# Cross attention of layer 1: one tile of values per chunk, a joint copy of the last chunk, layer norms moved behind a reciprocal

## Chip, cores and metric

The kernel runs on one core of a Trainium2 chip. The metric is the device time of one execution in microseconds. TensorE (PE in the profile, with its weight loads as PEld), VectorE (DVE), ScalarE (ACT) and GpSimd (POOL) each work through their own queue of instructions, and SyncE (SP) issues most of the DMAs.

## What is computed

The reference is a decoder of two layers on 32 sequences of 100 tokens with 256 features. Each layer has self attention, a cross attention to a context of 361 rows with 192 features, and a mixture of experts. The change touches the cross attention of layer 1 alone, and the code of that stage also starts the gating of the following mixture of experts. Cut to what matters:

```python
# x: (32, 100, 256), context: (32, 361, 192); 16 heads of 64
def _L1_xattn_ref(x, context, ln_gamma, ln_beta, Wq, Wkv, Wo, bo, mask):
    xn = (x - mu) * jax.lax.rsqrt(var + LN_EPS) * ln_gamma + ln_beta
    q = xn @ Wq
    k, v = jnp.split(context @ Wkv, 2, axis=-1)
    dots = jnp.einsum('bhnd,bhmd->bhnm', q, k) * scale      # q, k, v by head
    dots = jnp.where(mask, dots, -jnp.inf)
    attn = jax.nn.softmax(dots, axis=-1)
    out = jnp.einsum('bhnm,bhmd->bhnd', attn, v)            # back to (32, 100, 1024)
    return out @ Wo + bo

x = x + _L1_xattn_ref(_layernorm(x, axis=-1), ctx_768, ...)
x = x + _L1_ffn_ref(_layernorm(x, axis=-1), ...)            # experts; its gate reads the normed x
```

Everything is float32.

## The kernel before, in words

The stage works in units. Unit u is one sequence (u // 4) and four of its sixteen heads (u % 4), so there are 128 units. A loop calls `turn_of(n)` for n from -2 to 127, and one turn holds pieces of several units, one behind the other, so that each engine always has something to do. The order on TensorE, VectorE, ScalarE and GpSimd is the order in which the code is written: the stage stands in `in_order()`, which takes the order out of a scheduler's hands. The waits between engines are put in from what instructions read and write.

A turn n is, in order:

- `turn_weights`: twelve transposes of the weights of unit n (`ex`, made two turns earlier) into three `mm` tiles in PSUM, copied to `eT` by ScalarE, VectorE and ScalarE.
- `exponentials` of the second half of unit n + 1 on ScalarE.
- `part_of(n)`: work that isn't needed in every turn. When n is a multiple of 4, `finish` projects the sequence just done and adds it to x (VectorE), then adds a bias (GpSimd) and stores x. In certain turns of each 16 it does the layer norm of the next four sequences (`normed`: part 0 statistics, part 1 centering), their queries (`turned`, `queries`), and the gating of the four sequences just finished (`gating`: part 0 statistics, part 1 centering and a store to `xn_dram`, part 2 transposes, part 3 the gate's projection and the two best experts, part 4 the gates).
- `values(v, last, 0)`: the first half of the sums over the context's features for the values of a pair of units. The 361 rows of context fall into chunks of 128, 128 and 105. In an even turn the first two chunks are made, 512 columns each; in an odd turn (`last`) the third, as two halves of 256 columns. All go into one tile `sc` of PSUM, which has two parts of 512 columns.
- `keys(n + 3, 0)`, and `divided(n + 1)`: a reciprocal on VectorE of the sums of the weights (`rc`), and the multiplication of the weights by it on GpSimd.
- `values(v, last, 1)`: the second half of the sums, and then the copies out of `sc` into the tile `vb`: the first part by ScalarE (L1517), the second by VectorE (L1519).
- `scores(n + 2, 0)`: matmuls into the other of the two `sc` tiles, and VectorE lowers them into `s` with the row's extreme `nmx` (L1538). `keys(n + 3, 1)` with its copies into `kT` by ScalarE (L1484) and VectorE (L1485). `scores(n + 2, 1)`: these take the `sc` tile that the values were in.
- `sums`: 24 short matmuls of `eT` and `vb` into `po`, copied to `oT` by VectorE.

Statistics are four pairs of BATCH_NORM_STATS2 and BATCH_NORM_AGGREGATE and one small operation on VectorE, then a power on GpSimd (`rs`, L170). Centering is four TENSOR_SCALAR on VectorE (L176). PSUM is shared as two `sc` tiles, three `mm` tiles and one `po` tile.

The functions of the diff, with their callers:

Of the kernel before, what the change touches and what calls it, by code (L numbers as in the profile page):

```python
# [10 lines left out]
F32 = mybir.dt.float32  # L11
# [7 lines left out]
P = 128  # L19
# [3 lines left out]
NG = B // G  # L23
# [42 lines left out]
def kernel(ctx: ExitStack, tc: tile.TileContext, io: dict, out: bass.AP):  # L66
    nc = tc.nc
# [22 lines left out]
    def mm_tile():  # L90
        return psum["mm"][1].tile([P, 512], F32, tag="mm", name="mm")
# [29 lines left out]
    def bc(ap, axis, n):  # L121

        ap = ap.unsqueeze(axis)
        shape = list(ap.shape)
        shape[axis] = n
        return ap.to_broadcast(shape)
# [414 lines left out]
    with tc.tile_pool(name="x0", bufs=2) as pool, tc.tile_pool(name="x0p", bufs=1) as fixed:  # L541
# [32 lines left out]
        cbs, cns, cTs, kbs, kns, vbs, kTs, exs, eTs, oTs = {}, {}, {}, {}, {}, {}, {}, {}, {}, {}  # L574
# [188 lines left out]
        def divided(b):  # L763
            ex, sm = exs[b]
            rc = small.tile([T, XH], F32, tag="rc4", name="rc4")
            nc.vector.reciprocal(rc, sm)
            nc.gpsimd.tensor_tensor(ex, ex, bc(rc, 2, NK), ALU.mult)
# [54 lines left out]
        with in_order():  # L822
# [8 lines left out]
            for n in range(-4, B + 1):  # L831
# [18 lines left out]
                g = (n + 5) // G  # L850
# [4 lines left out]
                g = (n + 4) // G + 1  # L855
# [41 lines left out]
    with tc.tile_pool(name="f0", bufs=2) as pool:  # L897
# [40 lines left out]
        parts = {}  # L938
# [16 lines left out]
        def gating(g, part):  # L955
            if part == 0:
                x1T = pool.tile([P, 2, GT], F32, tag="x1T", name="x1T")
                transposed(x1T, x1s[g], tiles=mm_tile)
                pg = mm_tile()
                for i in range(G):  # L960
                    project(
                        pg[:T, i * E : (i + 1) * E],
                        [x1T[:, c, i * T : (i + 1) * T] for c in range(2)],
                        [f0_wg[:, c, :] for c in range(2)],
                    )
                lg = small.tile([T, G, E], F32, tag="lg", name="lg")
                nc.vector.tensor_tensor(
                    lg, pg[:T, : G * E].rearrange("p (g e) -> p g e", e=E),
                    bc(row("f0_gb"), 1, G), ALU.add,
                )  # L970
                nmx = small.tile([T, G], F32, tag="nmg", name="nmg")
                nc.vector.tensor_reduce(nmx, lg, AX.X, ALU.max, negate=True)
                nc.vector.tensor_tensor(lg, lg, bc(nmx, 2, E), ALU.add)
                nc.scalar.activation(lg, lg, AF.Exp)
                x1Ts[g], parts[g] = x1T, lg
                return
            lg = parts.pop(g)
            sm = small.tile([T, G], F32, tag="smg", name="smg")
            nc.vector.tensor_reduce(sm, lg, AX.X, ALU.add)
            nc.vector.reciprocal(sm, sm)  # L980
            gt = small.tile([T, G, E], F32, tag="gt", name="gt")
            nc.vector.tensor_tensor(gt, lg, bc(sm, 2, E), ALU.mult)
            _, hot = top2(pool, gt, G, row("iota", P))
            wt = small.tile([T, G, E], F32, tag="wt", name="wt")
            nc.vector.tensor_tensor(wt, hot[:T, 0], hot[:T, 1], ALU.add)
            nc.vector.tensor_tensor(wt, wt, gt, ALU.mult)
            wts[g] = [wt]
# [90 lines left out]
    with tc.tile_pool(name="a1", bufs=2) as pool, tc.tile_pool(name="a1p", bufs=1) as fixed:  # L1078
# [21 lines left out]
        for c in range(2):  # L1100
            ps = mm_tile()
# [5 lines left out]
        ps = mm_tile()  # L1107
# [213 lines left out]
        with in_order():  # L1321
            for part in range(11):
                project_group(0, part)
            for n in range(16 * NG + 12):
                g, at = n // 16, n % 16
# [79 lines left out]
    with tc.tile_pool(name="x1", bufs=2) as pool, tc.tile_pool(name="x1p", bufs=1) as fixed:  # L1405
# [32 lines left out]
        def normed(g, part):  # L1438
            if part == 0:
                lns[g] = stats(xs[g], G, twice=True, tag="l")  # L1440
            else:
                xn = pool.tile([T, G, D], F32, tag="xn", name="xn", bufs=1)
                centered(xn, xs[g], G, lns[g])
                lns[g] = xn
# [42 lines left out]
        def values(u, last, part):  # L1487

            b, v0 = u // 4, 512 * (u % 4 // 2)
            cT, vb = cTs[b], vbs[u // 2]  # L1490
            if last:
                k0, kn = CCH[2]
                parts = [(slice(k0, k0 + kn), kn, v0 + 256 * e, 256) for e in range(2)]
            else:
                parts = [(slice(k0, k0 + kn), kn, v0, 512) for k0, kn in CCH[:2]]
            if part == 0:
                held[u] = sc_tile()
            ps = held[u]
            for e, (at, kn, c0, n) in enumerate(parts):
                half = slice(64 * e, 64 * e + 64)  # L1500
                if part == 0:
                    nc.tensor.matmul(  # L1502
                        ps[:kn, e, :n], cT[:, 0, at], x1_wa[:, 1024 + c0 : 1024 + c0 + n],
                        start=True, stop=False,
                    )
                else:
                    nc.tensor.matmul(  # L1507
                        ps[:kn, e, :n], cT[half, 1, at], x1_wbv[half, c0 : c0 + n],
                        start=False, stop=True,
                    )  # L1510
            if part == 0:
                return
            for e, (at, kn, c0, n) in enumerate(parts):
                src = ps[:kn, e, :n].rearrange("p (h d) -> p h d", d=64)
                dst = vb[:kn, 2, 4 * e : 4 * e + 4, :] if last else vb[:kn, e, :, :]
                if e == 0:
                    nc.scalar.copy(dst, src)  # L1517
                else:
                    nc.vector.tensor_copy(dst, src)  # L1519

        def scores(u, c):

# [50 lines left out]
        def sums(u, eT, vb, oT):  # L1573

            q4 = u % 4
            po = po_tile()
            for m in range(2):
                for k, (k0, kn) in enumerate(CCH):
                    for e in range(2):
                        h = 2 * m + e  # L1580
                        nc.tensor.matmul(  # L1581
                            po[64 * e : 64 * e + 64, m * T : (m + 1) * T],
                            vb[:kn, k, 4 * (u % 2) + h, :], eT[:kn, k, h, :],
                            start=(k == 0), stop=(k == 2), tile_position=(0, 64 * e),
                        )
            nc.vector.tensor_copy(
                oT[:, 2 * q4 : 2 * q4 + 2, :].rearrange("p m t -> p (m t)"), po[:, : 2 * T]
            )
# [14 lines left out]
                small.tile([T, 4], F32, tag="sm4", name="sm4"),  # L1603
            )

        def value_tile():
            return pool.tile([P, 3, 8, 64], F32, tag="vb", name="vb")

# [3 lines left out]
        qTs, kTs, vbs, exs, oTs, held, lns, lowered = {}, {}, {}, {}, {}, {}, {}, {}  # L1614

        def part_of(n):

            g, at = n // 16, n % 16
            if n % 4 == 0 and n > 0:
                finish(n // 4 - 1, oTs.pop(n // 4 - 1))  # L1620
            if g + 1 < NG:
                if at in (1, 2):
                    normed(g + 1, at - 1)
                if at == 6:
                    lns[g + 1] = turned(lns[g + 1])
                    qTs[g + 1] = query_tile()
                if 7 <= at < 11:
                    for m in range(2):
                        queries(qTs[g + 1], lns[g + 1], 2 * (at - 7) + m)
            if n >= 18 and (n - 18) % 16 < 5:  # L1630
                gating(pool, (n - 18) // 16, (n - 18) % 16)

        def turn_of(n):
            if n >= 0:
                if n % 4 == 0 and n // 4 + 2 < B:
                    cTs[n // 4 + 2] = context(n // 4 + 2)
                eT = turn_weights(exs.pop(n)[0])
            if -1 <= n and n + 1 < NU:
                for e in range(2):
                    exponentials(n + 1, 1, e)  # L1640
            if n >= 0:
                part_of(n)
            v, last = n + 2 - n % 2, n % 2 == 1
            if v < NU:
                if not last:
                    vbs[v // 2] = value_tile()
                values(v, last, 0)
            if n + 3 < NU:
                keys(n + 3, 0)
            if -1 <= n and n + 1 < NU:  # L1650
                divided(n + 1)
            if v < NU:
                values(v, last, 1)
            if -2 <= n and n + 2 < NU:
                scores(n + 2, 0)
                exponentials(n + 2, 0, 0)
            if n + 3 < NU:
                keys(n + 3, 1)
            if -2 <= n and n + 2 < NU:
                exponentials(n + 2, 0, 1)  # L1660
                scores(n + 2, 1)
            if n >= 0:
                if n % 4 == 0:
                    oTs[n // 4] = pool.tile([P, 8, T], F32, tag="oT", name="oT", bufs=1)
                sums(n, eT, vbs[n // 2], oTs[n // 4])
# [46 lines left out]
    with tc.tile_pool(name="f1s", bufs=2, side="right") as pool, in_order(SP):  # L1712
# [154 lines left out]
        for n in range(len(units) + 2):  # L1867
            if n < len(units):
                h, m = units[n]
# [252 lines left out]
```

## Time and profile before

| | us |
|---|---|
| median of 3 runs | 3898.57 |
| lowest and highest run | 3896.55, 3901.43 |
| profiled execution, its own time | 3899.32 |
| its span in the profile | 3897.6 |
| the cross attention of layer 1, about | 1964 to 3182 |
| its turns n = 0 to 127, by the first transpose of each | 1973.1 to 3178.2 |

The profile shows one execution. A group's row reads: line, engine, operation, what is written and read, shapes and count | busy us, mean ns of one | idle us of the engine just ahead of it, and who ended that idle time. A row of the timeline reads: start in us, length in us, engine, line, operation, names and count, and in brackets the idle time ahead with its releaser. A row of busy time by stretch reads: the stretch and its length, then the busy us of PE, PEld, DVE, ACT and POOL with the count of instructions, the granted TensorE clock, the DMA engines' share and GB/s.

The turns repeat with a period of 16, since four sequences make a group: n % 16 tells what `part_of` does in the turn.

### The profile page before, as it was taken

What the parts mean: (1) busy time and instruction counts of PE and PEld (TensorE: products, weight loads), DVE (VectorE), ACT (ScalarE), POOL (GpSimd) and SP (SyncE); (2) the same over time, 40 slices, a digit from 0 to 9 for tenths busy, and PEclk for the clock granted to TensorE, in tenths of its full rate; (3) what the DMA queues carried; (4) which work ended last, traced back from release to release, by engine and by line L of the source; (5) the groups of instructions that cost most, each with busy time, mean ns of one, the idle gap of its engine ahead of it and who ended that gap; (6) DMA issues with size and microseconds to landing.
All of it is one profiled execution on the core that took longest, in us unless ns stands there. A gap on an engine that the chain in (4) does not pass through costs nothing. (4 is left out here: it accounts for less than half of the span.)

```text
span 3897.6 us, 65045 instructions
## 1 busy us (share of the span) xinstructions
PE 3581.0 (92%) x25566; PEld 2243.9 (58%) x25566; DVE 1962.1 (50%) x5533; ACT 1549.4 (40%) x3318; POOL 1329.7 (34%) x949
## 2 busy tenths in 40 slices
PE   7888999996889899799999999999999996999998
PEld 5665565554545453333356666666666665867675
DVE  6776666654677766565544454544544531012221
ACT  4554555553222220456644444444444441212121
POOL 3344666664444532101122232332322326012111
PEclk9999999998899989899999999999999998999999
DMA  2001000000000000400100000000000014512222
GB/s 79 2 2 58 18 20 20 18 5 15 1 1 1 1 1 0 122 1 1 34 10 16 15 20 11 20 16 15 16 15 16 15 46 140 165 35 34 34 35 57
DMA packets 94185, 110.18 MB, mean 28 GB/s; under 512 B 14142, under 2 KB 87430, under 8 KB 93290
## 3 DMA queue, kind: packets, MB, share of 16 engines
q1 hardware_dynamic: 79596, 88.40, 7.9%
q0 software_dynamic: 12304, 14.28, 2.3%
q8 instruction: 204, 3.34, 0.4%
q10 hardware_dynamic: 1982, 3.35, 0.3%
q14 instruction: 99, 0.81, 0.1%
HBM read 74.02 MB, written 35.23 MB: 28 GB/s over the span
## 5 line engine op out<-in xcount | busy, mean ns | idle before, releaser
L1556 POOL TENSOR_TENSOR ex<-ex,rc 100x1444 f32<-100x1444 f32 x128 | 331.9, 2593 | 492.7 <-DVE rc L1555 492.7
L1547 ACT ACTIVATE ex<-s,nmx 100x361 f32<-100x361 f32 x512 | 303.2, 594 | 145.4 <-DVE nmx L1538 145.4
L363 POOL TENSOR_TENSOR s<-s,nmx 100x800 f32<-100x800 f32 x128 | 194.7, 1522 | 378.1 <-DVE nmx L362 359.1
L1198 ACT ACTIVATE h<-sc,cols 128x800 f32<-128x800 f32 x256 | 222.3, 924 | 135.0 <-PE sc L1192 134.7
L207 PE MATMUL mm<-f_we,x1T 128*100 128x512 f32 x512 | 267.6, 654 | 4.3 <-DVE x L1008 2.3
L1538 DVE CUSTOM_DVE_ANT_0 s<-sc,mb 100x361 f32<-100x361 f32 x512 | 250.4, 528 | 0.1
L1519 DVE COPY vb<-sc 128x512 f32<-128x512 f32 (+1 forms) x128 | 71.5, 558 | 352.5 <-ACT vb L1517 352.5
L1974 POOL DMA_INDIRECT acc_dram<-y,xg x57 | 88.2, 1547 | 420.2 <-DVE y L1973 343.3
L1531 PE MATMUL sc<-kT,qT 64*100 64x361 f32 x1024 | 203.1, 473 | 13.0 <-DVE vb L1519 13.0
L207 PE MATMUL sc<-wx,xgT 128*128 x456 | 206.9, 597 | 0.3 <-DMA xg<-sorted_dram 0.3
L207 PE MATMUL po<-wx,hgT 128*128 x912 | 206.2, 379 | 0.3 <-ACT hgT L1956 0.3
L207 PEld LDWEIGHTS po<-wx,hgT 128*128 128x128 f32 x912 | 173.2, 190 | 47.9 <-issue 26.8
L170 POOL TENSOR_TENSOR rs<-va,neghalf 100x4 f32<-100x4 f32 (+1 forms) x96 | 92.7, 969 | 306.8 <-DVE va L169 217.8
L1973 DVE TENSOR_SCALAR y<-po,gx 128x256 f32<-128x256 f32 x57 | 27.6, 484 | 331.0 <-PE po L207 331.0
L1502 PE MATMUL sc<-x_wa,cT 128*128 128x512 f32 (+1 forms) x512 | 187.7, 489 | 0.0
L1517 ACT COPY vb<-sc 128x512 f32<-128x512 f32 (+1 forms) x128 | 61.3, 479 | 316.3 <-PE sc L1507 316.3
L1021 DVE SCALAR_TENSOR_TENSOR x<-mm,wt,x 100x256 f32<-100x256 f32 x256 | 123.6, 483 | 116.1 <-PE mm L207 109.7
L375 PE MATMUL mm<-ident,ex 100*100 100x100 f32 x1024 | 126.4, 262 | 58.9 <-ACT eT L384 22.7
L1472 PE MATMUL mm<-cT,x_wa 128*128 128x361 f32 x512 | 176.3, 467 | 0.0
L1581 PEld LDWEIGHTS po<-eT,vb 128*64 128x64 f32 (+1 forms) x3072 | 136.8, 137 | 67.3 <-issue 66.9
L1563 PE MATMUL mm<-ident,ex 100*128 100x100 f32 (+1 forms) x1536 | 163.6, 256 | 8.9 <-POOL ex L1556 8.2
L384 ACT COPY eT<-mm 100x400 f32<-100x400 f32 x192 | 92.4, 493 | 193.9 <-PE mm L375 193.4
(331 smaller groups left out, 7704.0 us busy)
## 6 DMA issues: line engine op xcount, KB each, us to landing
wx<-in_f_w SPq DMA_DIRECT2D x16, 1024.0 KB
sorted_dram<-empty SPq DMA_DIRECT2D x57, 132.5 KB
xg<-sorted_dram SPq DMA_DIRECT2D x57, 132.5 KB
cb<-in_ctx SPq DMA_DIRECT2D x32, 192.0 KB
cT<-in_ctxT SPq DMA_DIRECT2D x32, 180.5 KB
cT<-in_ctxT SPq DMA_DIRECT2D x64, 90.2 KB
x<-in_x SPq DMA_DIRECT2D x8, 400.0 KB
x_dram<-x SPq DMA_DIRECT2D x32, 100.0 KB
```

What stands on the lines that cost most here:

```text
L207: nc.tensor.matmul(ps, lhsT[k], rhs[k], start=(k == 0), stop=(k == n - 1))
L363: nc.gpsimd.tensor_tensor(sm, sm, bc(nmx, 2, T), ALU.add)
L375: nc.tensor.transpose(pt[:T, j * T : (j + 1) * T], exs[s, r // 2][:, 4 * (r % 2) + j, :], ident[:T, :T],)
L1198: nc.scalar.activation(h1, both[r2][:, :, :GT], AF.Tanh, bias=col("a1_b1", o))
L1472: nc.tensor.matmul(kTs[u][c][:, :S2], x1_wa[:, m * P : (m + 1) * P], cT[:, 0, :], start=True, stop=False,)
L1502: nc.tensor.matmul(ps[:kn, e, :n], cT[:, 0, at], x1_wa[:, 1024 + c0 : 1024 + c0 + n], start=True, stop=False,)
L1531: nc.tensor.matmul(ps[:T, e, :S2], qT[p0 : p0 + 64, m, tok], kT[p0 : p0 + 64, c, :], start=True, stop=True,)
L1538: nc.vector.tensor_tensor_reduce(s[:, e, :], ps[:T, e, :S2], mb, 1.0, 3.4e38, ALU.add, ALU.min, nmx[:, e : e + 1],)
L1547: nc.scalar.activation(ex[:, 2 * c + e, :], s[:, e, :], AF.Exp, bias=nmx[:, e : e + 1], scale=-1.0, accum_out=sm[:, 2 * c + e : 2 * c + e ...
L1556: nc.gpsimd.tensor_tensor(ex, ex, bc(rc, 2, S2), ALU.mult)
L1563: nc.tensor.transpose(pt[:kn, j * T : (j + 1) * T], ex[:, j, k0 : k0 + kn], ident[:T, :T])
L1581: nc.tensor.matmul(po[64 * e : 64 * e + 64, m * T : (m + 1) * T], vb[:kn, k, 4 * (u % 2) + h, :], eT[:kn, k, h, :], start=(k == 0), stop=( ...
```

## The change

It does four things. The tile `vb` with three chunks becomes three tiles of 512 columns, `vb0`, `vb1` and `vb2`, of which there are two each as before. The last chunk is copied out of `sc` by one VectorE instruction over both parts, where ScalarE and VectorE had a half each. The statistics and the centering, of `normed` as of `gating`, leave `part_of` and go to a new function `norms_of`, called behind `divided` and ahead of `values(v, last, 1)`. And their turns change: gating's five parts run at n % 16 = 1 to 5 where they ran at 2 to 6, the two parts of `normed` at 3 and 4 where they ran at 1 and 2.

```diff
             if part == 0:
                 return
-            for e, (at, kn, c0, n) in enumerate(parts):
-                src = ps[:kn, e, :n].rearrange("p (h d) -> p h d", d=64)
-                dst = vb[:kn, 2, 4 * e : 4 * e + 4, :] if last else vb[:kn, e, :, :]
-                if e == 0:
-                    nc.scalar.copy(dst, src)
-                else:
-                    nc.vector.tensor_copy(dst, src)
+            if last:
+                nc.vector.tensor_copy(vb[2][:kn].rearrange("p (e n) -> p e n", e=2), ps[:kn, :, :n])
+            else:
+                nc.scalar.copy(vb[0], ps[:, 0, :])
+                nc.vector.tensor_copy(vb[1], ps[:, 1, :])
...
-                            vb[:kn, k, 4 * (u % 2) + h, :], eT[:kn, k, h, :],
+                            vb[k][:kn, 256 * (u % 2) + 64 * h : 256 * (u % 2) + 64 * h + 64],
+                            eT[:kn, k, h, :],
...
-        def value_tile():
-            return pool.tile([P, 3, 8, 64], F32, tag="vb", name="vb")
+        def value_tiles():
+            return [pool.tile([P, 512], F32, tag=f"vb{k}", name=f"vb{k}") for k in range(3)]
...
             if g + 1 < NG:
-                if at in (1, 2):
-                    normed(g + 1, at - 1)
                 if at == 6:
...
-            if n >= 18 and (n - 18) % 16 < 5:
-                gating(pool, (n - 18) // 16, (n - 18) % 16)
+            if n >= 19 and 2 <= (n - 17) % 16 < 5:
+                gating(pool, (n - 17) // 16, (n - 17) % 16)
+
+        def norms_of(n):
+            g, at = n // 16, n % 16
+            if n >= 17 and at in (1, 2):
+                gating(pool, g - 1, at - 1)
+            if g + 1 < NG and at in (3, 4):
+                normed(g + 1, at - 3)
...
             if v < NU:
                 if not last:
-                    vbs[v // 2] = value_tile()
+                    vbs[v // 2] = value_tiles()
                 values(v, last, 0)
             if n + 3 < NU:
                 keys(n + 3, 0)
             if -1 <= n and n + 1 < NU:
                 divided(n + 1)
+            if n >= 0:
+                norms_of(n)
             if v < NU:
                 values(v, last, 1)
```

## The prediction, made before the result was known

> **What bounds the kernel now.** I start from the page: TensorE is busy for 92% of the span and no other engine for more than half, so a change helps only where TensorE stands still, and costs only where it makes TensorE stand still. Next, busy time by stretch: the stage that the diff touches runs from about 1964 to 3182 us, and TensorE is busy for 1196 of these 1218 us. The groups then name its two waits there.
>
> ```profile
> PE 3581.0 (92%) x25566; PEld 2243.9 (58%) x25566; DVE 1962.1 (50%) x5533; ACT 1549.4 (40%) x3318; POOL 1329.7 (34%) x949
> 1964.00:3182.00 1218.00, 1196.07 (x8611) 759.92 (x8610) 580.88 (x2057) 578.42 (x1612) 368.52 (x194) 1.00 0.06 15
> L1519 DVE COPY vb<-sc 128x512 f32<-128x512 f32 (+1 forms) x128 | 71.5, 558 | 352.5 <-ACT vb L1517 352.5
> L1531 PE MATMUL sc<-kT,qT 64*100 64x361 f32 x1024 | 203.1, 473 | 13.0 <-DVE vb L1519 13.0
> L1563 PE MATMUL mm<-ident,ex 100*128 100x100 f32 (+1 forms) x1536 | 163.6, 256 | 8.9 <-POOL ex L1556 8.2
> ```
>
> VectorE waits 352 us for the ScalarE copy of values, but VectorE is not the bound: TensorE lost 13 us to it, and 8 us to GpSimd's division. Ends of matmuls are modelled, so I read the real stalls from starts in the timeline, turn by turn. First an even turn (n = 46).
>
> ```profile
> 2418.60 1.13 PE L1507 MATMUL sc<-x_wbv,cT 64*128 64x512 f32 x4
> 2419.78 0.59 ACT L1517 COPY vb<-sc 128x512 f32<-128x512 f32 x1 [2.37 <-PE sc L1507]
> 2420.17 0.78 PE L1480 MATMUL mm<-cT,x_wbk 64*128 64x361 f32 x4
> 2420.39 0.69 DVE L1519 COPY vb<-sc 128x512 f32<-128x512 f32 x1 [2.71 <-ACT vb L1517]
> 2421.14 0.85 PE L1531 MATMUL sc<-kT,qT 64*100 64x361 f32 x4 [0.20 <-DVE vb L1519]
> ```
>
> The second scores need the sc tile that the values leave. The copies run one behind the other, the last ends at 2421.08, and the scores start 0.06 later: 0.97 after the keys' start. Now an odd turn (n = 45).
>
> ```profile
> 2410.60 0.18 DVE L1555 RECIPROCAL rc<-sm 100x4 f32<-100x4 f32 x1 [1.55 <-ACT ex L1547]
> 2411.94 0.77 PE L1480 MATMUL mm<-cT,x_wbk 64*128 64x361 f32 x4
> 2411.95 0.42 DVE L1519 COPY vb<-sc 105x256 f32<-105x256 f32 x1 [1.18 <-ACT vb L1517]
> 2412.55 0.77 PE L1531 MATMUL sc<-kT,qT 64*100 64x361 f32 x4
> 2413.20 0.53 DVE L1485 COPY kT<-mm 128x361 f32<-128x361 f32 x1
> 2413.52 0.44 ACT L1484 COPY kT<-mm 128x361 f32<-128x361 f32 x1
> ```
>
> Here the scores follow the keys after 0.61 with no wait: both copies ended by 2412.37. So only the 64 even turns lose 0.97 - 0.61 = 0.36, and 0.08 more because the scores themselves take 0.85 and not 0.77: 0.44 each, 28 us in all. The kT lines tell why the copies queue: both engines write one kT tile, from two mm tiles, and VectorE starts first with no wait. A shared destination orders nothing, so what orders the vb copies is their shared source, one sc tile. Last, the odd turn with norm statistics (n = 49).
>
> ```profile
> 2443.72 0.42 DVE L162 BATCH_NORM_STATS2 st<-x 100x6 f32<-100x256 f32 x1
> 2446.06 0.18 DVE L1555 RECIPROCAL rc<-sm 100x4 f32<-100x4 f32 x1
> 2446.23 1.03 POOL L170 TENSOR_TENSOR rs<-va,neghalf 100x4 f32<-100x4 f32 x1 [7.52 <-DVE rc L1555]
> 2449.88 0.91 PE L1563 MATMUL mm<-ident,ex 100*128 100x100 f32 x8 [0.61 <-POOL ex L1556]
> ```
>
> The statistics (2.34 us, 2443.72 to 2446.06) hold the reciprocal, the power on GpSimd (1.03) goes ahead of the division, and the next transposes wait. This turn lasts 7.59 us (2442.29 to 2449.88) and its twin n = 45 6.91. By the transposes' starts the same 0.68 recurs in 7 turns (n % 16 = 1), and 0.18 in 6 turns (n % 16 = 2, 8.85 against 8.67); n % 16 = 3 lasts a bare 6.91.
>
> **What the Trainium skill says.** "PSUM — Partial Sum Buffer", section "PSUM bank collisions raise a hardware error", says that two engines on one bank and quadrant must be kept apart, readers too, while different banks run clean. The halves of sc are 512 fp32 each, a bank by that page, so the chip would allow both copies at once; no trace here shows it done. The same page, "Engine vs sequencer instructions", calls VectorE's queue strict first-in first-out; the trace agrees (the reciprocal of n = 49 starts 0.70 later in its turn than that of n = 45). "Perfetto Trace Analysis", section "Identifying Dependency Chains", says that waits for several engines may add EventSemaphore instructions; the trace has three on TensorE here, 51 ns each.
>
> **The change part by part.**
> 1. Three tiles vb0, vb1, vb2 in place of one. In the list of the changed program's instructions all 64 copies vb1<-sc on VectorE still wait for the ScalarE copy vb0<-sc just ahead of them, as the kT reading says they must. The even turns stay as they are: 0 of the 28 us.
> 2. The last chunk is copied by VectorE alone: 64 ScalarE copies (0.37) and 64 VectorE copies (0.42) become 64 copies of 105x512. Nearest row: 128x512, 0.69. It starts when ScalarE's did (4.02 into the turn) and ends at 4.71 instead of 4.84; scores start at 5.02. Nothing gained, and nothing lost unless the copy takes over 0.95. What stands behind it on VectorE, the lowered scores, comes 0.1 earlier, and no row of the odd turns shows TensorE waiting for them: 0.
> 3. Norms behind the reciprocal. Removed: 7 x 0.68 + 6 x 0.18 = 5.8 us. Their new cover is VectorE's idle time ahead of the values' copy. Centering (four TENSOR_SCALAR, 1.3 us) falls into even turns: reciprocal 3.07 into the turn, centered at about 4.5, copy due at 5.95: hidden. The statistics fall into odd turns, and there the cover is too short. The reciprocal starts at 3.07 (2410.60 - 2407.53), the next instruction 0.09 later, the statistics take 2.34: the copy starts at 5.50 instead of 4.02 and ends at 6.19. Queued behind it on VectorE are the lowered scores, kT and oT; waiting for it is TensorE, whose second scores start at 6.24 instead of 5.02, and take the 0.08 more of a waiting start: 1.30 lost. The rest of VectorE's turn keeps its distance to TensorE, so the loss doesn't run on. The power now stands behind the division: POOL ends it 7.0 into an 8.2 us turn, in time for centering.
>  Which turns: gating statistics at n = 17, 33, ... 113 (7), layer norm statistics at n = 3, 19, ... 99 (7). From n = 19 on the turn also gets gating's 8 transposes, 0.72 us of TensorE work (12.99 against 12.27 where they were), so there 0.58 is left of the 1.30. Lost: 8 x 1.30 + 6 x 0.58 = 13.9 us.
> 4. Gating's other parts one turn earlier: the same TensorE work (0.72 and 1.58) in another turn. In n % 16 = 4 its VectorE chain ends about 8.6, centering about 9.9, ahead of a copy due at 11.1; the division ends near 11.6 of 13.85. The xn_dram store passes no other issue on SP; POOL's copies and iota go ahead of the division as before: 0.
> 5. New waits: the list has 52 more EventSemaphores on TensorE's queue (478 for 426), ahead of transposes, for things long done. Between 0 (the turn n = 45 has one ahead of its keys and is no longer than n = 51) and 52 x 51 ns = 2.7 us. I take 0 and keep 2.7 for the range.
>
> **Sum:** 13.9 - 5.8 = +8.1 us. The profiled execution took 3899.3 (span 3897.6), so 3907.4 for its like; the median of before lies 0.7 lower, at 3898.6: 3906.7, and I say 3907.
>
> **The rivals.** (a) *The copies of the even turns do run side by side.* VectorE would start at 2419.78 and end at 2420.47, ahead of TensorE's readiness at 2420.78, and all 28.2 us come: 28.2 - 8.1 = 20 faster, 3879. Faster from 19 turns on (8.1 / 0.44). For it: separate destinations, and banks that don't collide. Against it: the kT lines and the 64 waits in the list. (b) *The norms fit.* 352.5 us over 127 waits is 2.8 a turn, above 2.34: then only the 5.8 is seen, 3893, within 0.2%. Against it: the odd turn's wait is 1.18. (c) *The lateness runs on*, into the turns behind, with the 2.7 of semaphores: 14 x 0.5 + 2.7 on top, 3917.
>
> **How the numbers follow.** About 0.2% (7.8 us) is what can be told from no change. My case has 0.80, of which about a fifth falls under 7.8 (starts read to 0.05 us, 14 times): 0.64 slower, 0.16 same. (a) 0.05 faster. (b), whole or in part, 0.09 same. (c) 0.06 slower. The range runs from 3901, a third of my sum, to 3913, my sum with the semaphores and half of (c)'s rest; it leaves out (a) and about half of (b) and of (c), some 0.13.
>
> **What would show it.** Right: VectorE's copy 128x512 still waits about 245 us for ScalarE; turns with n % 16 = 1 (from n = 17) and n % 16 = 3 last 8.2; n % 16 = 2 8.67; pure even turns unchanged at 8.67; the transposes no longer wait for POOL. Wrong: pure even turns of 8.23 (a), or odd norm turns near 6.91 (b), or a longer turn behind them (c).

## The result: slower by 23.6 us, where 8 were forecast, and the profile after

| | before | after |
|---|---|---|
| median of 6 runs, us | 3898.07 | 3921.66 |
| ratio, 95% interval | | 1.0063 (1.0052 to 1.0073) |
| span of the profiled execution, us | 3897.6 | 3919.3 |
| turns n = 0 to 127 of the stage, us | 1205.1 | 1229.1 |

The direction was right. The size was three times what was forecast, and the time lies above the stated range of 3901 to 3913. The turns of the one stage account for all of it: 1229.1 - 1205.1 = 24.0 us.

The rows that the prediction read, now of the changed kernel. The two waits of TensorE, from its page:

```profile
L1529 PE MATMUL sc<-kT,qT 64*100 64x361 f32 x1024 | 204.3, 475 | 40.2 <-DVE vb L1517 24.6
...
L1561 PE MATMUL mm<-ident,ex 100*128 100x100 f32 (+1 forms) x1536 | 163.6, 256 | 3.9 <-POOL ex L1554 3.8
```

The busy time of the stretch that holds the stage (length, then PE, PEld, DVE, ACT, POOL):

```profile
1964.00:3206.00 1242.00, 1197.79 (x8610) 762.58 (x8607) 640.39 (x2057) 553.11 (x1547) 369.54 (x194) 1.00 0.05 15
```

The groups of the stage on VectorE, shapes kept apart, that the argument rests on:

```profile
L1517 DVE COPY vb<-sc 128x512 f32<-128x512 f32 x64 | 44.1, 689 | 210.1 <-ACT vb L1516 210.0
L1514 DVE COPY vb<-sc 105x512 f32<-105x512 f32 x64 | 44.0, 688 | 79.4 <-PE sc L1507 79.4
L176 DVE TENSOR_SCALAR xn<-x,mv,rs 100x256 f32<-100x256 f32 x28 | 26.2, 995 | 0.0
L176 DVE TENSOR_SCALAR x<-x,mv,rs 100x256 f32<-100x256 f32 x28 | 25.5, 973 | 0.0
L165 DVE TENSOR_SCALAR va<-mv 100x4 f32<-100x4 f32 x7 | 4.5, 639 | 0.2
L169 DVE TENSOR_SCALAR va<-mv 100x4 f32<-100x4 f32 x7 | 4.3, 618 | 0.2
```

The same groups in the kernel before, where the last chunk's copy had 105x256:

```profile
L1519 DVE COPY vb<-sc 128x512 f32<-128x512 f32 x64 | 44.3, 692 | 244.8 <-ACT vb L1517 244.8
L1519 DVE COPY vb<-sc 105x256 f32<-105x256 f32 x64 | 27.2, 425 | 107.7 <-ACT vb L1517 107.6
L176 DVE TENSOR_SCALAR xn<-x,mv,rs 100x256 f32<-100x256 f32 x28 | 9.6, 409 | 0.0
L176 DVE TENSOR_SCALAR x<-x,mv,rs 100x256 f32<-100x256 f32 x28 | 9.6, 409 | 0.0
L165 DVE TENSOR_SCALAR va<-mv 100x4 f32<-100x4 f32 x7 | 1.2, 171 | 0.2
L169 DVE TENSOR_SCALAR va<-mv 100x4 f32<-100x4 f32 x7 | 1.2, 170 | 0.2
```

Three things are to be seen. VectorE's copy of the even turns still waits 210 us for ScalarE's (244.8 before), so the separate tiles freed nothing. TensorE waits 40.2 us ahead of scores (13.0 before) and 3.9 ahead of transposes (8.9 before). And VectorE is busy for 640 us of the stage, not 581, with the same 2057 instructions. Of these 59 us the joint copy accounts for 17 (44.0 for 27.2), as it does ScalarE's half too. Most of the rest is in the norms: the centering takes 995 and 973 ns an instruction for 409, and the small operation of the statistics 639 and 618 for 171 and 170.

The timeline of a turn with centering (n = 50, 2456.54 to 2465.91, 9.37 us where 8.67 was forecast) shows when.

```profile
2459.55 0.18 DVE L1553 RECIPROCAL rc<-sm 100x4 f32<-100x4 f32 x1 [1.48 <-ACT ex L1545]
2459.64 3.65 DVE L176 TENSOR_SCALAR x<-x,mv,rs 100x256 f32<-100x256 f32 x4
2459.89 2.60 POOL L1554 TENSOR_TENSOR ex<-ex,rc 100x1444 f32<-100x1444 f32 x1 [4.86 <-DVE rc L1553]
2461.88 0.59 ACT L1516 COPY vb<-sc 128x512 f32<-128x512 f32 x1 [2.37 <-PE sc L1507]
2463.21 0.68 DVE L1517 COPY vb<-sc 128x512 f32<-128x512 f32 x1
2463.94 0.85 PE L1529 MATMUL sc<-kT,qT 64*100 64x361 f32 x4 [0.89 <-DVE vb L1517]
```

Four centering instructions, 1.3 us before, fill 3.65. Of the four, which the row merges, the second lasted 2.69 us, until 2462.64, and GpSimd's division ran until 2462.49. ScalarE had done its copy at 2462.47. VectorE comes to its own only at 2463.21, and the scores start 0.70 later than in a plain even turn. No row calls this a wait: the held instruction counts as busy.

The turn with statistics ahead of it (n = 49, 8.63 us):

```profile
2450.98 0.18 DVE L1553 RECIPROCAL rc<-sm 100x4 f32<-100x4 f32 x1 [1.55 <-ACT ex L1545]
2451.08 0.40 DVE L162 BATCH_NORM_STATS2 st<-x 100x6 f32<-100x256 f32 x1
2451.31 2.59 POOL L1554 TENSOR_TENSOR ex<-ex,rc 100x1444 f32<-100x1444 f32 x1 [6.97 <-DVE rc L1553]
2453.31 0.62 DVE L169 TENSOR_SCALAR va<-mv 100x4 f32<-100x4 f32 x1
2453.84 0.68 DVE L1514 COPY vb<-sc 105x512 f32<-105x512 f32 x1
2454.57 0.85 PE L1529 MATMUL sc<-kT,qT 64*100 64x361 f32 x4 [1.47 <-DVE vb L1514]
```

BATCH_NORM_STATS2 keeps its 0.40 beside the division. The TENSOR_SCALAR over four columns (the small operation) doesn't keep its 0.17: it ends at 2453.93, just after the division (2453.90).

### The profile page after: what moved, and what is told of

The parts are those of the page before. It is cut to its first block, busy times and chain, and to the rows that moved or that the text cites. A ratio compares the mean times of both kernels' runs of the same rounds, so it can differ in the third digit from the quotient of the medians.

```text
span 3919.3 us, 64989 instructions
## 1 busy us (share of the span) xinstructions
PE 3580.2 (91%) x25566; PEld 2246.0 (57%) x25566; DVE 2020.7 (52%) x5533; ACT 1524.8 (39%) x3254; POOL 1330.9 (34%) x949
## 5 line engine op out<-in xcount | busy, mean ns | idle before, releaser
L1529 PE MATMUL sc<-kT,qT 64*100 64x361 f32 x1024 | 204.3, 475 | 40.2 <-DVE vb L1517 24.6
L1568 ACT COPY eT<-mm 128x400 f32<-128x400 f32 (+1 forms) x256 | 125.9, 492 | 98.9 <-PE mm L1561 98.8
L1579 PE MATMUL po<-eT,vb 128*64 128x100 f32 (+1 forms) x3072 | 162.2, 254 | 0.0
```

Of the source, the lines that this page charges most:

```text
L1529: nc.tensor.matmul(ps[:T, e, :S2], qT[p0 : p0 + 64, m, tok], kT[p0 : p0 + 64, c, :], start=True, stop=True,)
L1579: nc.tensor.matmul(po[64 * e : 64 * e + 64, m * T : (m + 1) * T], vb[k][:kn, 256 * (u % 2) + 64 * h : 256 * (u % 2) + 64 * h + 64], eT[:kn ...
```

## The experiments

The theory is that VectorE's TENSOR_SCALAR from SBUF to SBUF stands still while GpSimd's division runs, and that the change put the norms exactly behind the reciprocal that starts the division. There are two rivals: the values' part of the change costs something, or the norms wait for something else (the stores of x, the power, their own data).

The runs were on several chips, on which the kernel before took 3898, 3916 or 3919 us (medians). So ratios count, each to the kernel before on the same chip. Beside them stands the sum of the turns, from the first transpose of turn 0 to that of turn 127. The last column has the length that recurs for each n % 16; it repeats to 0.02 us, and only the first or the last turn of a kind, in which other parts are at work, differs.

| kernel | ratio to before, 95% interval | turns, us | n % 16 = 1, 2, 3, 4 |
|---|---|---|---|
| before | | 1205.1 | 7.59, 8.85, 6.91, 12.98 |
| changed | 1.0063 (1.0052 to 1.0073) | 1229.1 | 8.63, 9.37, 8.59, 14.89 |
| values alone | 1.0003 (0.9995 to 1.0011) | 1203.8 | 7.58, 8.85, 6.91, 12.93 |
| norms alone | 1.0054 (1.0041 to 1.0067) | 1226.4 | 8.36, 9.37, 8.32, 14.89 |
| short division | 0.9997 (0.9988 to 1.0006) | 1208.4 | 8.18, 8.68, 8.11, 13.71 |
| centering first | 1.0029 (1.0018 to 1.0040) | 1217.1 | 8.63, 8.67, 8.59, 13.71 |
| centering with a sum | 1.0035 (1.0022 to 1.0047) | 1217.2 | 8.63, 8.68, 8.59, 13.71 |
| one-bank tiles | 0.9936 (0.9923 to 0.9949) | 1179.8 | 7.59, 8.85, 6.91, 12.54 |
| one-bank, norms fit | 0.9923 (0.9910 to 0.9936) | 1171.4 | 6.91, 8.23, 6.91, 11.82 |

### The two parts of the change apart

Values alone is the kernel before with the three tiles and the joint copy, and with the norms where they were.

```diff
+            if last:
+                nc.vector.tensor_copy(vb[2][:kn].rearrange("p (e n) -> p e n", e=2), ps[:kn, :, :n])
+            else:
+                nc.scalar.copy(vb[0], ps[:, 0, :])
+                nc.vector.tensor_copy(vb[1], ps[:, 1, :])
...
```

> The kernel before with the values' part alone: three tiles vb0, vb1, vb2 and the joint VectorE copy of the last chunk; the norms stay where they were. My theory: this part moves nothing, since VectorE's copy of the even turns still waits for ScalarE's; 3898 us, within 3 of before, even turns 8.67. Rival: a part of the 23.6 us lost comes from here (waits of the three tiles, the longer copy), then up to 3910. Second rival: the separate tiles free the copies, then 3870.

The runs show no difference (3915.6 against 3916.1), and even turns keep 8.67. The turns' sum is 1.3 us lower: turns that are multiples of four last 12.21 and not 12.27, as the projection of `finish` follows the transposes 0.05 sooner. Why it does was not tried.

Norms alone is the changed kernel with one `vb` and the two copies of the last chunk.

```diff
-            if last:
-                nc.vector.tensor_copy(vb[2][:kn].rearrange("p (e n) -> p e n", e=2), ps[:kn, :, :n])
-            else:
-                nc.scalar.copy(vb[0], ps[:, 0, :])
-                nc.vector.tensor_copy(vb[1], ps[:, 1, :])
+            for e, (at, kn, c0, n) in enumerate(parts):
+                src = ps[:kn, e, :n].rearrange("p (h d) -> p h d", d=64)
+                dst = vb[:kn, 2, 4 * e : 4 * e + 4, :] if last else vb[:kn, e, :, :]
...
```

> The changed kernel with the values' part undone: one tile vb, two copies of the last chunk; the norms behind the reciprocal as changed. My theory: all of the loss is here, 3921 us (22 to 25 over before), with turns n % 16 = 1, 2, 3, 4 of about 8.6, 9.4, 8.6, 14.9. Rival: the joint copy is a part of it, since in odd turns it makes VectorE later; then under 3915.

Nearly all of the loss is here, though a little less than the 22 expected at least: 1226.4 - 1205.1 = 21.3 us by turns, and 20.8 between the medians. The rival has a part. With the joint copy the odd norm turns are 0.27 longer (8.63 against 8.36, 8.59 against 8.32), since VectorE is late there and 0.69 is 0.27 more than 0.42. Over 14 turns that is 3.7 us; the turns with `finish` give about 1 back, so the joint copy's net part is 2.7 of the 24.0 us. It is free on its own and not free behind the statistics.

### Is it the division that holds VectorE?

This is the changed kernel, but GpSimd divides only 8 of the 361 columns of each head's weights. The others stay undivided, so only its times are read.

```diff
-            nc.gpsimd.tensor_tensor(ex, ex, bc(rc, 2, S2), ALU.mult)
+            nc.gpsimd.tensor_tensor(ex[:, :, :8], ex[:, :, :8], bc(rc, 2, 8), ALU.mult)
```

> The changed kernel, but GpSimd divides only the first 8 of each head's 361 columns of weights (the others stay undivided), so that its instruction is short and nothing else moves. Theory (VectorE's TENSOR_SCALAR stands still while GpSimd's division runs): centering takes 4 x 0.4 again and the statistics' small operation 0.17; turns n % 16 = 1, 2, 3 last 8.2, 8.67, 8.2, and the time is the recorded sum, 3907 us (3904 to 3909). Rival (they wait for something else: the stores of x, the power, their own data): turns of 8.6, 9.4, 8.6 stay, 3921.

The groups of its stage, GpSimd's division and VectorE's norms:

```profile
L1554 POOL TENSOR_TENSOR ex<-ex,rc 100x32 f32<-100x32 f32 x128 | 31.2, 244 | 844.3 <-DVE rc L1553 844.3
L176 DVE TENSOR_SCALAR xn<-x,mv,rs 100x256 f32<-100x256 f32 x28 | 9.9, 413 | 0.0
L176 DVE TENSOR_SCALAR x<-x,mv,rs 100x256 f32<-100x256 f32 x28 | 9.6, 407 | 0.0
L169 DVE TENSOR_SCALAR va<-mv 100x4 f32<-100x4 f32 x7 | 1.2, 171 | 0.2
L165 DVE TENSOR_SCALAR va<-mv 100x4 f32<-100x4 f32 x7 | 1.2, 170 | 0.2
```

With a division of 0.24 us in place of 2.59, centering is back at 0.41 and the small operation at 0.17, in the same place and behind the same stores. The power comes earlier here, as it stands behind the division, but it can't have been what centering waited for: in the changed kernel the power of n = 49 ended at 2455.04, and the centering of n = 50 starts at 2459.64. So the rival of another wait falls. The turns are those of the prediction: 8.18, 8.68 and 8.11 for 8.2, 8.67 and 8.2. The time itself was missed: 3907 expected, 3897 measured (before: 3898). Of the missing 10 us some 5 can be read from the turns: turn 126, near the end, lasts 3.64 and not 5.99, as it no longer waits for a division, and the turns that are multiples of four are 0.05 to 0.14 shorter than in my sum, n % 16 = 3 0.10. The rest, some 4 us between the stage's +3.3 and the ratio's -1.1 (-4.7 to +2.3), lies outside the stage and stays open. In the profiled executions on that chip the stage began at 1967.7 us in this kernel and at 1973.6 in the next one, with the same code ahead of it: single executions differ there by more than is missing.

### Is it the order or the form of the instruction?

This is the changed kernel with the two centerings ahead of the reciprocal again, in their new turns.

```diff
+            if n >= 17 and at == 2:
+                gating(pool, g - 1, 1)
             if g + 1 < NG:
+                if at == 4:
+                    normed(g + 1, 1)
...
-            if n >= 17 and at in (1, 2):
-                gating(pool, g - 1, at - 1)
-            if g + 1 < NG and at in (3, 4):
-                normed(g + 1, at - 3)
+            if n >= 17 and at == 1:
+                gating(pool, g - 1, 0)
+            if g + 1 < NG and at == 3:
+                normed(g + 1, 0)
```

> The changed kernel with the two centerings put back ahead of the reciprocal, in the same turns as changed (n % 16 = 2 and 4); the statistics stay behind it. Theory: TENSOR_SCALAR there runs ahead of the division, so n % 16 = 2 lasts 8.67 and n % 16 = 4 13.85, which gives 7 x 0.70 + 6 x 1.04 = 11 us back: 3910 us; the statistics' 0.62 stays. Rival (centering holds the reciprocal and with it the next transposes, as the statistics did): less than 5 back, over 3916.

As expected: 3910.6 against 3897.9, n % 16 = 2 back at 8.67 and n % 16 = 4 at 13.71, 12.0 us of turns. Ahead of the reciprocal the centering adds nothing to these turns, although in seven of them (n % 16 = 4) one centering instruction took 0.82, held beside GpSimd's addition of the bias. So it is not the division alone that holds it.

The next is the changed kernel with centering in the same place behind the reciprocal, but in another form, which also writes a sum that nobody reads.

```diff
+            more = {} if sums is None else {"accum_out": sums[:np_, i : i + 1]}
             nc.vector.tensor_scalar(
                 dst[:, i, :], src[:, i, :], mv[:np_, i, 0:1], rs[:np_, i : i + 1],
-                ALU.subtract, ALU.mult,
+                ALU.subtract, ALU.mult, **more,
             )
...
```

> The changed kernel, with the eight centering instructions of a group given an accumulator output that nobody reads; same place, same data, same waits. The skill's page on SBUF says that a tensor_scalar which also writes its accumulator has no mode on two ports, and so should not compete with GpSimd. Theory (the hold is the shared port): centering takes about 4 x 0.4 to 0.6 beside the division, turns n % 16 = 2 and 4 fall to 8.67 and 13.7, the statistics' small operation keeps its 0.62, and the time is about 3911 us, as with the centering ahead of the reciprocal. Rival (any TENSOR_SCALAR from SBUF to SBUF waits for GpSimd, whatever its mode): 9.4 and 14.9 stay, 3921.

With this form the stored values differ, so only its times are read.

The instructions that write the tile `xn`, first of the changed kernel, then of this one (count, then shortest, median and longest duration in ns, and first and last start):

```profile
L176 DVE TENSOR_SCALAR xn<-x,mv,rs x28: 380/402/2748, 2009.1 to 2959.8; 100x256 f32<-100x256 f32 x28
L177 DVE TENSOR_SCALAR_CACHE_REDUCE xn<-x,mv,rs x28: 507/534/539, 2019.3 to 2957.9; 100x256 f32<-100x256 f32 x28
```

None of the 28 is held, and the longest lasts 539 ns, beside the same division, where the plain form had up to 2748. Nor is one of the other 28, those of gating (533 to 540). The turns are those of the kernel above, to 0.01 us. The statistics' small operation, whose form wasn't changed, keeps its 0.64. Place and waits being equal, the form decides. The Trainium skill says why: "SBUF — State Buffer", section "Who interferes with whom", has VectorE and GpSimd share one pair of SBUF ports, which a `tensor_scalar` may take in its two-port modes; whoever has it first keeps it for the whole instruction, and the form with an accumulator output doesn't take it. The runs show VectorE's plain form held by GpSimd and the other form free. That it is that port is the page's word, and the runs don't show GpSimd held in its turn: the divisions that began 0.15 us before a centering instruction ended took 2.60, the others 2.59.

### What orders the copies

This is the kernel before with `sc` in this stage as two tiles of one bank. The scores' matmuls and the reads of them are changed in the same way.

```diff
-                held[u] = sc_tile()
+                held[u] = sc_halves()
...
+        def sc_halves():
+            return [psum["s1"][1].tile([P, 512], F32, tag="s1", name="s1") for _ in range(2)]
...
-                src = ps[:kn, e, :n].rearrange("p (h d) -> p h d", d=64)
+                src = ps[e][:kn, :n].rearrange("p (h d) -> p h d", d=64)
...
```

> The kernel before, with each sc tile of two banks cut into two tiles of one bank (four in all in place of two); vb stays one tile, the norms stay. What the prediction says of the order of the copies: the shared source orders them. Then both copies of an even turn start together, 64 turns lose their 0.44, and the time is 3898 - 28 = 3870 us (up to 3873, as PSUM is parted anew behind the stage), even turns 8.23. Rival: the destination vb, or the chip itself, orders them: 3898, even turns 8.67.

Its timeline in an even turn (n = 46):

```profile
2402.06 1.13 PE L1510 MATMUL s<-x_wbv,cT 64*128 64x512 f32 x4
2403.22 0.59 ACT L1520 COPY vb<-s 128x512 f32<-128x512 f32 x1 [2.35 <-PE s L1510]
2403.26 0.69 DVE L1522 COPY vb<-s 128x512 f32<-128x512 f32 x1 [2.12 <-PE s L1510]
2404.23 0.77 PE L1534 MATMUL s<-kT,qT 64*100 64x361 f32 x4
```

Both copies start together, 0.04 apart, into one and the same `vb`, and the scores take 0.77 with no wait. Even turns last 8.23. So the shared source orders the copies, as the prediction had read, and neither the destination nor the chip does. Of the 28 us 25.3 came, since the six turns with n % 16 = 2 stayed at 8.85: their next transposes wait for the division (11.7 us on TensorE in this kernel), which the shorter turn doesn't hasten.

The last kernel is the same with the norms where the profile has room: statistics behind the reciprocal of turns that are multiples of four (`statistics_of` is called behind `divided`), centering in `part_of`, ahead of the reciprocal, one turn later.

```diff
+        def statistics_of(n):
+            g, at = n // 16, n % 16
+            if at == 4 and g + 1 < NG:
+                normed(g + 1, 0)
+            if at == 8 and n >= 16:
+                gating(pool, g - 1, 0)
...
+                if at == 5:
+                    normed(g + 1, 1)
+            if n >= 16 and at in (9, 11, 12, 13):
+                gating(pool, g - 1, {9: 1, 11: 2, 12: 3, 13: 4}[at])
```

> As the kernel with one-bank tiles, and the norms put where they fit: the statistics behind the reciprocal, but in turns that are multiples of four (n % 16 = 4 and 8), where the reciprocal is at 5.3 and the copy of values near 9; the centering ahead of the reciprocal in the odd turns behind them (n % 16 = 5 and 9); gating's other parts at 11, 12, 13. My theory: the 0.68 of 7 turns and the 0.18 of 6 go, 5.8 us under the one-bank kernel: 3864 us. Rival: the small operation of the statistics is held until GpSimd's division ends at about 8.9 and delays the copy: then no more than 2 under it.

The busy time of its stage, and behind it the small operation of the layer norm's statistics (durations in ns as above):

```profile
1964.00:3151.00 1187.00, 1182.80 (x8623) 775.11 (x8622) 612.06 (x2057) 577.71 (x1612) 369.58 (x194) 1.00 0.06 15
```

```profile
L165 DVE TENSOR_SCALAR va<-mv x7: 1146/1150/1154, 2011.2 to 2908.5; 100x4 f32<-100x4 f32 x7
```

Half of the rival came true: the small operation is held, for 1.15 us now, until the division ends. But in these turns the copy comes later still (in n = 52 the held operation ends at 8.80 and the copy starts at 8.96), so the hold costs nothing: n % 16 = 4 lasts 11.82, as the turns without norms do.

By the busy time of its stretch, TensorE is idle for 4 us in the stage. The turns give 8.4 us over the one-bank tiles, more than the 5.8 expected, because the six turns at 8.85 now get the 0.44 too. The medians lie 3.8 apart (3883.96 and 3887.74), not enough to tell the two kernels from each other by time alone. Against the kernel before it is 0.77% faster (0.64 to 0.90). By its turns it is the version to keep.

## Why the prediction was right or wrong

Steps 1, 2 and 5 of the working held, and step 4 but for its centering. The 64 copies vb1<-sc waited on, and the reading behind it, that the shared source orders them and not the destination, is shown by the one-bank tiles. The joint copy took 0.688 (0.69). Gating's other parts moved without a trace: n % 16 = 5 fell from 8.49 to 6.91, as they left it. The extra EventSemaphores cost nothing that a turn shows (pure odd turns 6.91); the "three on TensorE here" are those of scores and sums alone, and the whole stage has 35 before and 87 after. Of step 3, the placing of the statistics held: the turn n = 49 has its reciprocal at 3.07, and with a short division the turns come out as written.

What failed is the cost of the moved norms. In step 3 it is "Centering (four TENSOR_SCALAR, 1.3 us) falls into even turns [...] hidden", and with it the 2.34 for the statistics; in step 4 it is the same price again, "centering about 9.9, ahead of a copy due at 11.1". In the changed kernel the four took 3.65 us in n = 50 and 3.7 in n = 52, there until 12.26 into the turn; in n = 49 the copy starts 2.76 behind the statistics' start. Both durations came from a trace in which none of these TENSOR_SCALAR ran beside a GpSimd instruction, and the move put them beside the 2.6 us of a division that starts 0.3 behind the same reciprocal. The prediction said nothing of what GpSimd's work does to VectorE's. By turns, in us:

| n % 16 | forecast | measured | difference, and its cause |
|---|---|---|---|
| 1 | +4.3 | +7.3 | 3.0: small operation 0.62 for 0.17 |
| 2 | -1.1 | +3.8 | 4.9: centering 3.65 for 1.3, 7 x 0.70 |
| 3 | +9.8 | +12.6 | 2.8: small operation 0.64 |
| 4 | +6.0 | +12.1 | 6.1: centering 3.7 for 1.3, 6 x 1.18; less 7 x 0.14, forecast too long |
| 5 | -11.1 | -11.1 | 0 |
| others | 0 | -0.8 | `finish` 0.05 sooner |

16 us in all, which takes the 8.1 to 24. VectorE was held for 32 us in centering ((995 - 409) + (973 - 409) ns, 28 times each) and for 6 in small operations ((639 - 171) + (618 - 170), 7 times each). What of this lay in VectorE's idle time didn't reach TensorE. In the turn n = 4 nothing did: its reciprocal comes at 5.3, the held centering ends at 9.40, and the copy is due at 9.50. In n = 20, 36 and so on gating's chain puts the reciprocal at 8.5, and the hold runs past the copy.

That the forecast had the right sign is owed to the one cost that it did see, the statistics in the odd turns. Rival (c) came nearest to the measured time, with 3917, but by luck: its mechanism is lateness that runs into the turns behind, and the turns n % 16 = 5 behind the worst ones last a bare 6.91.

## What to carry to other kernels

Before an instruction is moved into another engine's idle time, look at what the *other* engines do in that window, not only whether its own engine is free there: its duration was measured beside something else. The hold showed here as a longer busy time with no releaser, so compare mean durations of the same row before and after. A hold need not be avoided where there is room for it: 1.15 us in a long turn cost nothing. Where two engines copy out of one PSUM tile, look at the order of their waits: cutting the source, and not the destination, freed them here.

## What the runs showed of the hardware

VectorE's TENSOR_SCALAR from SBUF to SBUF stood still while GpSimd's TENSOR_TENSOR ran, at either size. For 100x4 it took 618 to 639 ns on average in the changed kernel and up to 1154 in the last one, where it takes 170 alone; for 100x256 up to 2748, where it takes 402. The held ones ended 0.02 us (100x4) and 0.15 us (100x256) behind GpSimd's instruction. One that had started 0.25 to 0.31 us ahead of the division was not held (0.38 to 0.40); one whose recorded start fell within 0.01 of the division's was (2.75). BATCH_NORM_STATS2 was not held (0.39 to 0.43 beside the division, as without it), nor were VectorE's copies out of PSUM (0.69 for 128x512 either way). The form with an accumulator output wasn't either (507 to 540 ns), and costs 534 ns and a read of 82 in place of 402. ScalarE and VectorE read two one-bank tiles of PSUM at once with their usual durations, 0.59 and 0.69.
